# A transformer's cross-attention on one core: where a query's logits bank, a grouped output's projection and a norm's squares stand in the order of work

## The chip, the cores and the metric

The kernel runs on one core of one Trainium2 chip. The metric is the device time of one execution in microseconds; the median of three runs is used. PE is the matrix engine (its weight loads are shown as PEld), DVE the vector engine, ACT the scalar engine, POOL the general engine, SP the queue that issues most transfers.

## The reference

Four cross-attention layers follow each other on x (4 batches, 512 rows, 256 wide), all with the same context (4 batches, 1024 rows, 512 wide). Layers 0, 2 and 3 are alike: 16 heads of 64, a bias of -20 on some key columns by two masks, and a residual. Layer 1 is grouped: an RMS norm first, 16 query heads of 16 wide that share 4 key heads.

```python
def masked_layer(x, ctx):                 # layers 0, 2, 3
    q, k, v = x @ Wq, ctx @ Wk, ctx @ Wv  # 16 heads of 64
    logits = q k^T / 8 + col_bias
    return softmax(logits) v @ Wo + bo + x

def grouped_layer(x, ctx):                # layer 1
    xn = x * rsqrt(mean(x * x) + 1e-5) * norm_w
    q, k, v = xn @ wq, ctx @ wk, ctx @ wv # 16 and 4 heads of 16
    return x + softmax(q k^T / 4) v @ wo
```

## The kernel before

**Units and steps.** Each layer of a batch is cut into eight units: two heads of a masked layer, or half of four query heads of the grouped one. `order()` lays the 96 masked units out one to a step, and the 32 grouped units of layer 1 beside some of them: in steps 11 to 18, 21 to 28, 31 to 38 and 67 to 74. In the main loop (line 953) `g` is the step's masked unit, `lam` its grouped unit, `g1` the masked unit of the step before, `follows` and `coming` the masked and grouped units of the next step, `soon` the grouped unit of the step after that. A step with `lam` is called a grouped step here. Of a run's eight grouped units, two after each other (`h` 0 and 1) make one output; when the second is done, it is put in `turned` and in the next step's outputs.

**A step's work.** The scores of `g` come first (line 622): for eight blocks of 128 keys PE makes logits (L632, in the first block the bias too, L638), ACT copies them to SBUF (L642), DVE keeps a running maximum (L646) in the bank of the first block. DVE then reduces that maximum (L683 to L716), and spreads it over a pair of banks (`max_everywhere`, L723). The attention of `g1` (L662) is PE's next work. In a grouped step it is cut in four, and behind each quarter stand the second logits of `lam` (`exponentials_pair`, L611 on PE, L619 on ACT): the first ones were made in the step before by `maxima_pair` (L611, L601 and L603), and `lower_queries` (L709) took their maximum off the queries. DVE meanwhile works out the reciprocal sums of `g1` (L791 to L803), the normalised grouped output if `turned` has one (L779 to L785), and scales the output of `g1` (L814).

**What is woven in.** The rest of a step's PE work is in the list `fill`, with an estimated time for each item: output projections (L829, whose addition to x is DVE's L851), query projections (L543, scaled by ACT in L549 or, grouped, L553 with a transfer each in L554), the attention of `lam`, key projections (L467, grouped L485; ACT copies them out in L472 and L492), the norm (L575, L582, L586, L565 to L590), the context's transposes, and values (L509, L521). A clock `now` adds these estimates up. The subtractions of the maximum (L728 on DVE) and the exponentials (L734 on ACT) are events with due times on that clock; an item's own ending on ACT or DVE is issued behind the events that are due. The maxima pairs of `coming` have due times too, and are put ahead of the next item when these have passed. `behind_exponentials` issues all events that are left, and the normalisation of `g1` where that was put off.

```python
        now = 0.0
        for us, w in fill:
            while pairs and pairs[0][0] <= now:
                pair(pairs.pop(0)[1])
                now += 1.0
                pairs = [(max(at, now + 1.6), i) for at, i in pairs]
            done = w()
            now += us
            if callable(done):
                pass_events(now)
                done()
```

**Banks.** All eight banks of PSUM are handed out by `Place` (line 96). It takes the bank, or the even-odd pair, that was given back first, counted by returns in the order of the program; `back(late=n)` counts a bank as given back n returns later. A single bank whose partner is free counts two later. A matmul into a bank waits until the bank's last reader is done.

[...]

Of the kernel before, what the change touches and what calls it, by code (L numbers as in the profile page):

```python
# [20 lines left out]
NT = T // P  # L21
# [55 lines left out]
def kernel(ctx: ExitStack, tc: tile.TileContext, a: dict, out: bass.AP):  # L77
# [8 lines left out]
    def t_(shape, tag, name, bufs=1, dtype=FP):  # L86
        return sb.tile(shape, dtype, tag=tag, name=name, bufs=bufs)
# [31 lines left out]
    def st_slot(n):  # L119
        return st_all[:, n // (NT + 1), n % (NT + 1), :]  # L120
# [197 lines left out]
    def new_state(l, b):  # L318
        x_at[l, b] = x_free.pop(0)
        xs[l, b] = x_all[:, x_at[l, b]]  # L320
        return xs[l, b]

    def drop_state(l, b):
        x_free.append(x_at[l, b])
# [131 lines left out]
    def k_part(g, n, part):  # L456

        if not g.masked:
            return k_grouped(g, n, part)
        if n == 0 and part == 0:  # L460
            g.kt = t_([P, T], "kt", f"kt_{g.name}", bufs=2)
        if part == 0:
            g.k_place = Place(1)
        w = g.k_place
        m = w.ap
        for k in (2 * part, 2 * part + 1):
            nc.tensor.matmul(  # L467
                m, lhsT=g.wk[:, k, :], rhs=ctx_t[g.b][:, k, n * 512 : (n + 1) * 512],
                start=(k == 0), stop=(k == KT - 1),
            )  # L470
        if part:
            return lambda: (nc.scalar.copy(g.kt[:, n * 512 : (n + 1) * 512], m), w.back())  # L472
# [60 lines left out]
    def project_q(g):  # L533
        if g.masked:
            g.qt = t_([P, S], "qt", f"qt_{g.name}", bufs=2)
        else:
            g.qts = [t_([P, S], f"qt1{i}", f"qt1{i}_{g.name}", bufs=2) for i in range(2)]
            g.qt = g.qts[0]
        x = xs[g.l, g.b] if g.masked else gq[g.b, "xn"]
        w = Place(1)  # L540
        m = w.ap
        for k in range(KC):
            nc.tensor.matmul(m, lhsT=g.wq[:, k, :], rhs=x[:, k, :], start=(k == 0), stop=(k == KC - 1))  # L543
        if g.masked and g.last:
            drop_state(g.l, g.b)

        def evacuate():
            if g.masked:
                nc.scalar.mul(g.qt, m, 0.125)  # L549
            else:  # L550
                for h in range(2):
                    here, there = (slice(64 * i, 64 * (i + 1)) for i in (h, 1 - h))
                    nc.scalar.mul(g.qts[h][here, :], m[here, :], 0.25)  # L553
                    nc.scalar.dma_start(out=g.qts[h][there, :], in_=g.qts[h][here, :])  # L554
            w.back()

        return evacuate

    def reciprocal_rows(out_, in_, room):


        turned = room[:, 0:S]
        short = t_([P, S // 32, 1], "short", f"short{len(turns)}")
        turns.append(0)
        nc.vector.transpose(turned, in_)  # L565
        nc.vector.reciprocal(short, turned.rearrange("p (c r) -> p c r", r=32)[:, :, 0:1])
        nc.vector.transpose(
            out_.rearrange("p (c r) -> p c r", r=32), short.to_broadcast([P, S // 32, 32])
        )
# [3 lines left out]
    def norm_square(b):  # L573
        gq[b, "xn"] = t_([P, KC, S], "xn", f"xn{b}")
        nc.scalar.activation(gq[b, "xn"], xs[1, b], AF.Square)  # L575

    def rms_norm(b, room):
        x, xn, nw = xs[1, b], gq[b, "xn"], columns["L1_xattn_norm_w"]
        w = Place(1)
        m = w.ap  # L580
        for k in range(KC):
            nc.tensor.matmul(m, lhsT=ones, rhs=xn[:, k, :], start=(k == 0), stop=(k == KC - 1))  # L582

        def evacuate():
            inv = t_([P, S], "stage", f"inv{b}")
            nc.scalar.activation(inv, m, AF.Sqrt, bias=eps, scale=1.0 / C)  # L586
            w.back()
            reciprocal_rows(inv, inv, room)
            for k in range(KC):
                nc.vector.scalar_tensor_tensor(  # L590
                    xn[:, k, :], x[:, k, :], nw[:, k : k + 1], inv, ALU.mult, ALU.mult
                )

        return evacuate
# [222 lines left out]
    def project_out(g):  # L817
        x, acc = xs[g.l, g.b], xs.get((g.l + 1, g.b))
        opens = acc is None
        if opens and g.masked:  # L820
            acc = new_state(g.l + 1, g.b)
        elif opens:

            acc = xs[g.l + 1, g.b] = x
            x_at[g.l + 1, g.b] = x_at[g.l, g.b]
        w = Place()
        m = w.ap
        for k in range(KC):
            nc.tensor.matmul(  # L829
                m[:, k * S : (k + 1) * S], lhsT=g.wo[:, k * P : (k + 1) * P], rhs=g.ot,  # L830
                start=True, stop=True,
            )
        y = m.rearrange("p (k q) -> p k q", q=S)

        def add_last(q):
            nc.vector.tensor_tensor(acc[:, :, q], y[:, :, q], acc[:, :, q], ALU.add)

        def add():
            if g is masked[-1]:
                for i in range(0, NI, 2):  # L840
                    add_last(slice(i * P, (i + 2) * P))
                    store(g.b, range(i, i + 2))
                left[g.b] = -1
            elif opens and g.masked:
                bo = columns[f"L{g.l}_xattn_bo"]
                for k in range(KC):
                    nc.vector.scalar_tensor_tensor(
                        acc[:, k, :], y[:, k, :], bo[:, k : k + 1], x[:, k, :], ALU.add, ALU.add
                    )
            else:  # L850
                nc.vector.tensor_tensor(acc, y, x if opens else acc, ALU.add)  # L851
            w.back()

        left[g.b] -= 1
        return add
# [85 lines left out]
    def keys(of):  # L941
        return [(1.7, lambda h=h, part=part: k_part(of, h, part)) for h in range(2) for part in range(2)]
# [5 lines left out]
    count = 0  # L948
# [4 lines left out]
    for n in range(len(steps) + 2):  # L953
        g, lam = at(n)
        follows, coming = at(n + 1)
        soon = at(n + 2)[1]
# [29 lines left out]
        outs, ready = ready, []  # L986
        events = []
        late = []
# [6 lines left out]
        def behind_exponentials():  # L995
            pass_events(99.0)
            while late:
                late.pop(0)()
# [15 lines left out]
        queries = []  # L1014
# [19 lines left out]
        if turned or lam and g1:  # L1034

            w = Place(1)
            if lam and g1:
                reciprocal_sums(g1, w.ap)
            for each in turned:
                normalise_grouped(each, w.ap)  # L1040
            w.back()
        turned.clear()
        if lam:
            for i in range(NT // 2):
                if g1:
                    attend(g1, range(2 * i, 2 * i + 2))
                if coming and not g:
                    pair(i)
                exponentials_pair(lam, i)
                if i == 0 and g:  # L1050
                    g.mx_place.back()
                if not g:
                    if i == 1 and outs:
                        project_out(outs.pop(0))()
                    if i == 2 and queries:
                        project_q(queries.pop(0))()
            if g1:
                scale_out(g1)
                ready.append(g1)
            if g:  # L1060
                max_everywhere(g)
        elif g1 and g:
            attend(g1)
            if not ending:
                late.append(lambda: normalise(g1))
        elif g1:
            attend_last(g1)
            adds = [project_out(each) for each in outs]
            outs = []
            reciprocal_rows(g1.ot, g1.psum, g1.mx)  # L1070
            scale_out(g1)
            for add in adds:
                add()
# [9 lines left out]

        fill = [(1.8, lambda each=each: project_out(each)) for each in outs]
        outs = []
        of_queries = [(1.7, lambda each=each: project_q(each)) for each in queries]
        if lam:

            fill[0:0] = of_queries[0:1]
            fill += of_queries[1:]
        else:
            fill += of_queries
        if lam:

            def attend_grouped():
# [8 lines left out]
        for of in kk:  # L1106
            fill += keys(of) if of else []
        if soon and soon.first:
            fill += keys(soon)
        if follows and follows.l and follows.u == 0:  # L1110
            fill.append((1.7, lambda: project_q(follows)))
        if soon and soon.first:

            def norm():
                behind_exponentials()
                norm_square(soon.b)
                return rms_norm(soon.b, st_slot((NT + 1) * (count % 2) + NT))

            fill.append((1.7, norm))
        fill += [(1.0, rest) for rest in rests]  # L1120
        if coming and coming.first:
            fill += values(coming)
# [60 lines left out]
```

## Time and profile before

| what | value |
|---|---|
| runs of the kernel | 3748.72, 3751.1 (median), 3751.64 us |
| the profiled execution | 3749.48 us |
| its span | 3747.7 us |
| granted clock of PE | 0.996 |
| busy: PE, PEld, DVE, ACT, POOL | 98%, 49%, 81%, 56%, 43% |
| transfers | 98.59 MB, 26 GB/s over the span |

The span runs from the first to the last instruction of the profiled execution. A step can be read off the timeline from its first L632 to the next step's. A plain step takes 31.94 us (from 1788.51, for one); the grouped steps that begin at 1517.02 and 1562.81 take 45.79 and 51.64 us. The former finds nothing in `turned`, the latter does.

### The profile page before, as it was taken

Reading aid. Unit: us, or ns where it says so; the run is one execution under the profiler, and the core shown is the slowest. Engines: PE = TensorE matmul, PEld = TensorE weight load, DVE = VectorE, ACT = ScalarE, POOL = GpSimd, SP = SyncE. Lnnn points to the kernel's source line nnn. Section 1 sums busy time; section 2 is a strip of 40 time slices with the busy share of each in tenths; the row PEclk is TensorE's granted clock in tenths of the full one; section 3 lists DMA queues with packets and bytes.
Section 4 is the critical chain, followed back from the end, with each engine's and each line's share of the span. In section 5 each row is a group of like instructions: output and inputs, shape, how many; then the busy total and the mean of one; then the engine's idle time right before and its main releaser. Section 6 shows DMA issues by size and latency. Waiting matters only on the chain.

```text
span 3747.7 us, 48412 instructions
## 1 busy us (share of the span) xinstructions
PE 3683.2 (98%) x18606; PEld 1836.7 (49%) x18606; DVE 3025.1 (81%) x3959; ACT 2109.2 (56%) x2433; POOL 1625.9 (43%) x749
## 2 busy tenths in 40 slices
PE   8999999999999999999999999999999999999998
PEld 4555544445444454444555555554544445555554
DVE  6887788877888778887788878888788877888887
ACT  4555566555555555555555655555555555555554
POOL 3555433343333433334455555555333344555554
PEclk9999999999999999999999999999999999999999
DMA  2111110001000010000000110000100000000100
GB/s 68 43 32 25 40 30 22 18 20 25 22 22 18 21 25 22 19 21 18 26 26 26 48 37 26 26 23 22 25 22 22 18 24 26 26 26 26 31 25 8
DMA packets 187868, 98.59 MB, mean 26 GB/s; under 512 B 43240, under 2 KB 183528, under 8 KB 187636
## 3 DMA queue, kind: packets, MB, share of 16 engines
q1 hardware_dynamic: 182510, 82.90, 8.0%
q0 software_dynamic: 2560, 8.39, 0.8%
q10 hardware_dynamic: 2566, 4.20, 0.5%
q8 instruction: 147, 2.41, 0.3%
q14 instruction: 85, 0.70, 0.1%
HBM read 89.16 MB, written 2.10 MB: 24 GB/s over the span
## 4 chain that ended last, share of the span: by engine, by line
PE 89%; DVE 8%; ACT 1%; issue 1%; DMA 0%; POOL 0%; DVEq 0%; ACTq 0%; POOLq 0%
PE ps L509 19%; PE ps L662 18%; PE ps L467 17%; PE ps L632 15%; PE ps L611 6%; PE ps L829 5%; PE ps L543 5%; DVE ps L646 4%; DVE st L728 1%; ACT st L642 1%; PE ps L485 1%; PE ps L638 1%; DVE quarter L683 1%; DVE ps L683 0%; PE ps L373 0%
## 5 line engine op out<-in xcount | busy, mean ns | idle before, releaser
L773 POOL TENSOR_TENSOR st<-st 128x1024 f32<-128x1024 f32 x668 | 1581.2, 2367 | 2059.6 <-ACT st L734 2015.4
L646 DVE TENSOR_TENSOR ps<-ps,st 128x1024 f32<-128x1024 f32 x672 | 828.6, 1233 | 483.4 <-ACT st L642 422.1
L734 ACT ACTIVATE st<-st 128x1024 f32<-128x1024 f32 x768 | 788.4, 1055 | 668.6 <-DVE st L728 652.1
L728 DVE TENSOR_TENSOR st<-st,ps 128x1024 f32<-128x1024 f32 x768 | 886.3, 1216 | 3.2
L662 PE MATMUL ps<-st,v 128*64 128x512 f32 x4064 | 810.9, 598 | 0.0
L509 PEld LDWEIGHTS ps<-wv,ctx 128*128 128x128 f32 x6400 | 729.4, 192 | 80.9 <-issue 63.8
L642 ACT COPY st<-ps 128x1024 f32<-128x1024 f32 x768 | 713.1, 1049 | 68.6 <-PE ps L638 67.5
L509 PE MATMUL ps<-wv,ctx 128*128 128x128 f32 x6400 | 744.8, 276 | 0.6 <-ACT st L642 0.6
L632 PE MATMUL ps<-qt,kt 64*128 64x512 f32 x3072 | 702.5, 596 | 0.3 <-ACT st L642 0.3
L467 PE MATMUL ps<-ctx,wk 128*128 128x512 f32 x1536 | 694.9, 600 | 2.2 <-ACT ctx L379 2.2
L662 PEld LDWEIGHTS ps<-st,v 128*64 128x64 f32 x4064 | 231.2, 130 | 551.5 <-issue 460.5
L467 PEld LDWEIGHTS ps<-ctx,wk 128*128 128x128 f32 x1536 | 286.6, 191 | 398.0 <-issue 375.0
L632 PEld LDWEIGHTS ps<-qt,kt 64*128 64x128 f32 x3072 | 284.5, 186 | 324.4 <-ACT st L642 155.6
L521 ACT COPY v<-ps 128x512 f32<-128x512 f32 x200 | 117.3, 586 | 540.9 <-PE ps L509 537.0
L603 DVE TENSOR_TENSOR st<-st,ps 128x1024 f32<-128x1024 f32 x224 | 273.6, 1221 | 118.7 <-ACT st L601 65.9
L619 ACT ACTIVATE st<-ps 128x1024 f32<-128x1024 f32 x256 | 248.2, 1021 | 155.3 <-PE ps L611 114.9
L611 PE MATMUL ps<-qt,kt 32*128 32x512 f32 x2048 | 308.0, 639 | 3.2 <-DVE ot L814 3.2
L829 PE MATMUL ps<-ot,wo 128*128 128x512 f32 x448 | 218.2, 614 | 11.1 <-issue 10.3
L543 PE MATMUL ps<-x,wq 128*128 128x512 f32 x384 | 186.8, 609 | 16.6 <-DVE ot L785 15.5
L611 PEld LDWEIGHTS ps<-qt,kt 32*128 32x128 f32 x2048 | 93.2, 183 | 179.1 <-ACT st L619 51.9
L472 ACT COPY kt<-ps 128x512 f32<-128x512 f32 x192 | 110.3, 574 | 93.2 <-PE ps L467 92.3
L829 PEld LDWEIGHTS ps<-ot,wo 128*128 128x128 f32 x448 | 79.8, 190 | 141.2 <-issue 134.8
(142 smaller groups left out, 1573.3 us busy)
## 6 DMA issues: line engine op xcount, KB each, us to landing
wk<-in_L_xattn_Wk_dram SPq DMA_DIRECT2D x96, 256.0 KB
wv<-in_L_xattn_Wv_dram SPq DMA_DIRECT2D x96, 256.0 KB
wq<-in_L_xattn_Wq_dram SPq DMA_DIRECT2D x96, 128.0 KB
wo<-in_L_xattn_Wo_dram SPq DMA_DIRECT2D x96, 128.0 KB
qt<-qt ACTq DMA_DIRECT2D x32, 128.0 KB
xraw<-in_x_dram SPq DMA_DIRECT2D x3, 512.0 KB
out_dram<-out SPq DMA_DIRECT2D x3, 512.0 KB
wq<-in_L_xattn_wq_dram SPq DMA_DIRECT2D x32, 32.0 KB
```

Source lines behind the costliest of these rows:

```text
L467: nc.tensor.matmul(m, lhsT=g.wk[:, k, :], rhs=ctx_t[g.b][:, k, n * 512 : (n + 1) * 512], start=(k == 0), stop=(k == KT - 1),)
L509: nc.tensor.matmul(m[:, t * P : (t + 1) * P], lhsT=ctx_t[g.b][:, k, (4 * n + t) * P : (4 * n + t + 1) * P], rhs=g.wv[:, k, :], start=(k == ...
L543: nc.tensor.matmul(m, lhsT=g.wq[:, k, :], rhs=x[:, k, :], start=(k == 0), stop=(k == KC - 1))
L611: nc.tensor.matmul(ws[odd].ap[:, j * S : (j + 1) * S], lhsT=g.kt[rows, i * P : (i + 1) * P], rhs=g.qt[rows, :], start=True, stop=True,)
L632: nc.tensor.matmul(m[:, j * S : (j + 1) * S], lhsT=g.kt[g.rows[j], keys], rhs=g.qt[g.rows[j], :], start=True, stop=t > 0,)
L642: nc.scalar.copy(g.st[t], m)
L646: nc.vector.tensor_tensor(top, top, g.st[t], ALU.max)
L662: nc.tensor.matmul(g.po[at, :], lhsT=g.v[:, t, rows], rhs=g.st[t][:, j * S : (j + 1) * S], start=(t == first), stop=(t == last),)
L728: nc.vector.tensor_tensor(g.st[t], g.st[t], g.mb, ALU.subtract)
L734: nc.scalar.activation(st, st, AF.Exp)
L773: nc.gpsimd.tensor_tensor(g.acc, g.st[0] if t == 1 else g.acc, g.st[t], ALU.add)
L829: nc.tensor.matmul(m[:, k * S : (k + 1) * S], lhsT=g.wo[:, k * P : (k + 1) * P], rhs=g.ot, start=True, stop=True,)
```

## The change

Three things are moved.

First, in grouped steps the first query projection is issued directly behind the last of the second logits, before the output of `g1` is scaled and before `max_everywhere` takes its banks; it is no longer the first item of `fill`, and adds nothing to `now`. With it, the bank in which the reciprocal sums and the normalised grouped output are worked out is given back with `late=12`.

Second, in the step behind a run of grouped steps (19, 29, 39 and 75), the projection of the grouped output that was normalised in that step is put behind the keys, and behind the query.

Third, in the four steps with a norm (9, 19, 29 and 65) the squares are issued behind the third of the four grouped key parts, with the events that are left ahead of them; the norm's matmul stays behind the keys, and in steps 19 and 29 behind the moved projection.

```diff
-            w.back()
+            w.back(late=12)
         turned.clear()
...
                     if i == 2 and queries:
                         project_q(queries.pop(0))()
+            if g and queries:
+                project_q(queries.pop(0))()
             if g1:
                 scale_out(g1)
                 ready.append(g1)
...
-        fill = [(1.8, lambda each=each: project_out(each)) for each in outs]
+        fill, of_grouped = (
+            [(1.8, lambda each=each: project_out(each)) for each in outs if lam or each.masked == m]
+            for m in (True, False)
+        )
+        if lam:
+            of_grouped = []
         outs = []
         of_queries = [(1.7, lambda each=each: project_q(each)) for each in queries]
-        if lam:
-
-            fill[0:0] = of_queries[0:1]
-            fill += of_queries[1:]
-        else:
-            fill += of_queries
+        fill += of_queries
...
         if soon and soon.first:
-            fill += keys(soon)
+            def square():
+                behind_exponentials()
+                norm_square(soon.b)
+            of_keys = keys(soon)
+            fill += of_keys[:3] + [(0.0, square)] + of_keys[3:]
+        fill += of_grouped
         if follows and follows.l and follows.u == 0:
             fill.append((1.7, lambda: project_q(follows)))
         if soon and soon.first:
-            def norm():
-                behind_exponentials()
-                norm_square(soon.b)
-                return rms_norm(soon.b, st_slot((NT + 1) * (count % 2) + NT))
-            fill.append((1.7, norm))
+            fill.append((1.7, lambda: rms_norm(soon.b, st_slot((NT + 1) * (count % 2) + NT))))
```

## Prediction

> **What bounds the kernel now.** I read the page's busy times first, then the waits of PE, then the timeline step by step.
>
> ```profile
> PE 3683.2 (98%) x18606; PEld 1836.7 (49%) x18606; DVE 3025.1 (81%) x3959; ACT 2109.2 (56%) x2433; POOL 1625.9 (43%) x749
> ```
>
> PE sets the end; only 3747.7 - 3683.2 = 64.5 us are left in which it idles. The change removes no matmul, so all it can give is a part of these, and all it can take is new waits. PE's waits (line, releaser: total us, times, longest):
>
> ```profile
> PE ps L543 <- DVE ot L785: 15.5, 10, 1.6
> PE ps L829 <- issue: 10.3, 4, 2.6
> PE ps L582 <- ACT xn L575: 6.9, 4, 1.7
> ```
>
> These are the three things that the change speaks of: a query projection (L543) in a bank that the normaliser (L785) still reads; a grouped output's projection (L829) that needs the normalised output; the norm's matmul (L582) behind its squares. From start to start of matmuls in the timeline, where 128x512 ones follow each other every 0.43 us, they cost 1.77 us (12 times with two under "issue", one of them 1.2: 20.8 in all), 2.74 us (4 times: 11.0) and 1.90 us (4 times: 7.6). I use these.
>
> A step with a grouped unit ("grouped step"), timeline, first where the last step finished a grouped pair ("turned" is set):
>
> ```profile
> 537.57 0.69 DVE L785 TENSOR_TENSOR ot<-o,ps 128x512 f32<-128x512 f32 x1
> ...
> 538.32 1.98 PE L543 MATMUL ps<-x,wq 128*128 128x512 f32 x4 [1.58 <-DVE ot L785]
> ...
> 540.14 3.60 PE L829 MATMUL ps<-ot,wo 128*128 128x512 f32 x8
> ```
>
> and one where it is not:
>
> ```profile
> 489.98 1.25 DVE L723 STREAM_TRANSPOSE ps<-every 128x1024 f32<-128x1024 f32 x1
> ...
> 490.17 1.94 ACT L619 ACTIVATE st<-ps 128x1024 f32<-128x1024 f32 x2 [1.01 <-PE ps L611]
> ...
> 491.82 1.88 PE L829 MATMUL ps<-ot,wo 128*128 128x512 f32 x4
> ```
>
> To see here: the second logits' last exponential ends at 492.11, 0.29 us after the output projection starts, and DVE's L723 starts before either of the last two exponentials is done.
>
> [...] the trace has 1.28 us before the root (L586), but no load before the square (L575), so moving the square adds none.
>
> **The change, part by part.**
>
> *1. Banks of the query (late=12, query ahead of scale_out).* PE's order stays: the query was the first of fill already. Only the bank changes. I followed the allocator by hand through a turned and an unturned step. Before, the query takes the single bank that reciprocal_sums just gave back; L723 takes the oldest pair (sixth exponential), the output projection the pair of the seventh. After, that single bank counts twelve returns later, so the query takes half of the oldest pair, which ACT has read. Gain: 12 x 1.73 = 20.8 us.
>
> But a pair is now broken up, so each later taker moves on by one: L723 gets the seventh exponential's pair, the output projection the eighth's. PE then waits until 492.11 + 0.06 instead of 491.82: 0.35 us, and as much in turned steps (eighth exponential 538.77, projection due at 538.4). 32 x 0.35 = 11.2 us lost. L723 waits from 489.98 to 491.2; behind it on DVE stand eight subtractions, the output addition, keep_odd and the maxima. The last subtraction ends at about 503.3 (eight at 1.15 us, one addition); the first maxima pair, which takes its bank, is due at 504.5 to 504.9: covered. Without that cover it costs up to 1.2 us a step (rival D).
>
> *2. The 1.7 us that vanish from fill's clock.* The query no longer counts in `now`, so maxima pairs, due at 12.0 + 2.5 i, come one item later, and events one item later too. In turned steps that helps: in six of them the first pair waits 0.7 us for the last subtraction (pair to next key matmul 1.75 instead of 1.05): 6 x 0.7 = 4.2 us gained. In unturned steps it hurts. By fill's costs (1.8 output, 3.6 attend, four keys at 1.7) the fourth pair now has one value item behind it, not two. Before:
>
> ```profile
> 512.47 1.14 PE L611 MATMUL ps<-qt,kt 32*128 32x512 f32 x8
> ...
> 517.31 1.13 PE L632 MATMUL ps<-qt,kt 64*128 64x512 f32 x4
> ...
> 519.35 0.75 DVE L709 SCALAR_TENSOR_TENSOR qt<-ps,row,qt 128x512 f32<-128x512 f32 x1
> ```
>
> From the fourth pair (512.47) to the end of L709 (520.10) it is 7.63 us of PE, then DVE. The next scores' fourth block, which takes L709's bank in nearly all these steps, is due 4.84 + 2.89 = 7.73 us after the pair: just in time. With one value item (1.9 us) less it is due at 5.85. If it takes that bank, scores end 1.8 us late; if it takes another and the fifth block takes it, 0.97 us (one step of before, at 615.5, has this order and loses 0.6). The three unturned steps with maxima and no second query in each of four runs: 12 x 1.35 (middle) = 16.2 us lost; 11.6 to 21.6. Eight other grouped steps come to the old margin of 0.1 us: 0.2 each, 1.6 (0 to 4.8).
>
> Sum of 1 and 2: -20.8 - 4.2 + 11.2 + 16.2 + 1.6 = +4.0 us (-3 to +14).
>
> *3. Grouped output behind the keys (steps 19, 29, 39, 75).* PE goes on with query and keys while DVE normalises (L785 ends 2.7 us after the turn of the first projection; the keys alone give 6.9). Step 19: -2.74. Step 29 has 1.8 us of further bank waits beside it (48.9 us against 47.2 for the same items): -3.5 (2.7 to 4.5). Step 39: the same 1.8 us, but the first value item then comes at the bank of the second key half 0.7 us early: -3.7. Step 75 goes the other way:
>
> ```profile
> 3080.10 3.12 PE L829 MATMUL ps<-ot,wo 128*128 128x512 f32 x4 [2.58 <-issue]
> ...
> 3085.58 5.74 DVE L728 TENSOR_TENSOR st<-st,ps 128x1024 f32<-128x1024 f32 x5
> ...
> 3090.46 1.88 PE L543 MATMUL ps<-x,wq 128*128 128x512 f32 x4
> ```
>
> There the next item, project_q(follows), opens layer 2 of the same batch and reads the x that this output completes. By then fill's clock has issued all eight subtractions ahead of the addition (L851), which ends at about 3091.4; the query starts there, not at 3090.46, though PE could at 3085.9. +1.0 (0 to +2). Sum: -8.9 us (-7 to -11).
>
> *4. Squares amid the keys (steps 9, 19, 29, 65).* Before, ACT's key copy (0.69) and square (1.05) follow the last key part, then PE starts: 1.9 us. After, the square stands ahead of that copy, and 1.7 us of key matmuls lie beside it. ACT's exponentials end at 834.2, before the third part (835.9 to 837.6), so the square is done near 837.9 and L582 due at 839.4. Gain 4 x 1.9 = 7.6 us (6 to 7.6). The late normalise goes to DVE one item earlier: nothing waits. If ACT were behind, the second key copy would be too; nobody needs it before the next step.
>
> **Queues.** No DMA is moved: grouped queries keep their two on ACT's queue (L554) directly behind their scaling; SP's weight loads stand between steps; POOL's sums only follow exponentials that come at most 1.2 us later, and POOL is busy 43%.
>
> **Sum.** +4.0 - 8.9 - 7.6 = -12.5, call it -13 us. On the profiled execution: 3749.5 - 13 = 3736.5 (its span of 3747.7 and 1.8 around). That execution lies 1.6 us under the median, so on the median 3751.1 - 13 = 3738. The likeliest case's own range is 3731 to 3745.
>
> **Rivals.**
> - A, forecast: new waits take the place of the query's. 3738, chance 0.55.
> - B, one or both new waits don't appear (the blocks find other banks). Without L709's, -13 - 17.8 = -31: 3720; without the eighth exponential's, -24: 3727; without both, 3710. For it: each hangs on bank numbers, and ties decide some. Against: there are only four pairs, and the scores use all within four blocks. Chance 0.20.
> - C, losses at their upper ends and waits like L611 on L814 (three of 1.25 us now, by luck of banks) come more often: +10 on A, about 3748, no change to speak of. Chance 0.16.
> - D, slower: L723's 1.2 us reach PE at the first maxima pair, in the 20 unturned steps: 20 x 1.2 = 24, 3762. It breaks even at 0.65 us a step and is measurable from 1.0. For it: in turned steps that pair waits on just this subtraction today. Against: the pair comes 1.7 us later now, and 1.2 to 1.6 us of margin remain. Chance 0.09.
> - That the query keeps its bank is excluded: twelve returns exceed the nine between.
>
> **Numbers.** A measurement of this kernel can tell some 0.2% (7.5 us) from no change. Faster: A but its edge (0.51) and B (0.20), 0.71; same: that edge and C, 0.20; slower 0.09. The range takes in C and B but for its end: 3720 to 3749.
>
> **What would show it.** L543 on L785 gone from PE's waits; L829 on L619 in 32 steps at 0.3 us; the scores (L632) waiting on L709 in 12 steps; grouped steps in pairs as long as now (97.4 us for 45.79 + 51.64); step 9 and 65 shorter by 1.9, step 19 by 4.6, step 29 by 5 to 6; step 75 longer by 1, with its query waiting on L851. It is wrong if pairs of grouped steps shorten by over 1 us or lengthen by over 3.

## The result: no difference that can be measured, and the profile after

The changed kernel takes 3748.6 us (median of 14 runs, 3746.54 to 3749.53), the kernel before 3749.97 us in as many runs beside it. The ratio is 0.9995, with a 95% interval of 0.9987 to 1.0003. The interval takes in 1, so not even the sign of a difference is shown. The forecast of 3738 is missed by 11 us; the measured time lies 0.4 us inside the upper end of the range, where case C stood.

What the change set out to remove is gone. PE's waits in the changed kernel (line, releaser: total us, times, longest):

```profile
PE ps L632 <- DVE qt L709: 6.4, 7, 1.7
PE ps L829 <- ACT st L619: 5.5, 32, 0.2
PE ps L543 <- ACT st L734: 5.3, 1, 5.3
PE ps L632 <- ACT st L642: 4.7, 14, 0.3
```

None of the three lines of before is left. In their place stand the scores behind L709, the output projection behind the eighth exponential (32 times, as many as there are grouped steps) and one query that waits 5.3 us. The page shows how little such sums tell: PE's busy time rose from 3683.2 to 3694.7 us with the same 18606 matmuls. In L632 alone it rose from 702.5 to 714.3 us, with 3072 matmuls in both, so a part of the new waits shows as busy time.

```profile
PE 3694.7 (99%) x18606; PEld 1842.0 (49%) x18606; DVE 3033.9 (81%) x3959; ACT 2105.5 (56%) x2433; POOL 1624.2 (43%) x749
```

So I compare step by step, from a step's first L632 to the next one's. The steps not named here agree within 0.1 us.

| steps | before to after, us |
|---|---|
| 32 grouped steps, sum | +12.4 |
| of these, with something in turned (12) | -0.3 |
| 9 and 65 (squares alone) | -3.6 |
| 19 (both) | -4.6 |
| 29 and the step behind it (both) | -6.7 |
| 39 and 40 (grouped output) | -3.0 |
| 75 and 76 (grouped output) | +3.9 |
| all | -1.6 |

The span fell by 3.0 us (the profiled execution after is the fastest of its fourteen); the rest lies before the first step and in the last one and behind it, which the change leaves alone. The new waits, in the timeline of the changed kernel. First an unturned step:

```profile
488.59 1.94 ACT L619 ACTIVATE st<-ps 128x1024 f32<-128x1024 f32 x2 [1.01 <-PE ps L611]
...
489.64 1.26 DVE L723 STREAM_TRANSPOSE ps<-every 128x1024 f32<-128x1024 f32 x1 [1.48 <-ACT st L619]
...
490.58 1.98 PE L829 MATMUL ps<-ot,wo 128*128 128x512 f32 x4 [0.17 <-ACT st L619]
```

L723 starts when the first of the last two exponentials is done (489.6), L829 when the second is (490.53). Then the start of the turned step behind it:

```profile
513.11 1.14 PE L611 MATMUL ps<-qt,kt 32*128 32x512 f32 x8
514.18 2.05 PE L509 MATMUL ps<-wv,ctx 128*128 128x128 f32 x16
...
516.16 1.13 PE L632 MATMUL ps<-qt,kt 64*128 64x512 f32 x4
...
520.00 0.75 DVE L709 SCALAR_TENSOR_TENSOR qt<-ps,row,qt 128x512 f32<-128x512 f32 x1
...
520.89 4.56 PE L632 MATMUL ps<-qt,kt 64*128 64x512 f32 x20 [1.67 <-DVE qt L709]
```

One value item (16 matmul records) now stands between the fourth maxima pair and the scores, not two, and the fourth block waits until L709 has let its bank go: 7.64 us behind the pair, as before.

### The profile page after: what moved, and what is told of

Its sections match the earlier page's. It is cut to its first block, busy times and chain, and to the rows that moved or that the text cites. A ratio compares the mean times of both kernels' runs of the same rounds, so it can differ in the third digit from the quotient of the medians.

```text
span 3744.7 us, 48356 instructions
## 1 busy us (share of the span) xinstructions
PE 3694.7 (99%) x18606; PEld 1842.0 (49%) x18606; DVE 3033.9 (81%) x3959; ACT 2105.5 (56%) x2433; POOL 1624.2 (43%) x749
## 4 chain that ended last, share of the span: by engine, by line
PE 90%; DVE 6%; ACT 2%; issue 1%; DMA 0%; POOL 0%; DVEq 0%; ACTq 0%; POOLq 0%
PE ps L662 20%; PE ps L509 19%; PE ps L467 17%; PE ps L632 16%; PE ps L611 8%; PE ps L829 5%; PE ps L543 3%; DVE ps L646 2%; DVE st L728 1%; ACT st L642 1%; ACT st L619 1%; PE ps L485 1%; PE ps L638 1%; DVE quarter L683 1%; DVE st L603 0%
## 5 line engine op out<-in xcount | busy, mean ns | idle before, releaser
L734 ACT ACTIVATE st<-st 128x1024 f32<-128x1024 f32 x768 | 783.0, 1054 | 706.3 <-DVE st L728 695.0
L509 PE MATMUL ps<-wv,ctx 128*128 128x128 f32 x6400 | 752.8, 277 | 1.2 <-ACT st L642 0.6
L632 PE MATMUL ps<-qt,kt 64*128 64x512 f32 x3072 | 714.3, 598 | 11.1 <-DVE qt L709 6.4
L467 PE MATMUL ps<-ctx,wk 128*128 128x512 f32 x1536 | 685.6, 597 | 2.2 <-ACT ctx L379 2.2
L632 PEld LDWEIGHTS ps<-qt,kt 64*128 64x128 f32 x3072 | 290.4, 186 | 340.9 <-ACT st L642 155.1
L619 ACT ACTIVATE st<-ps 128x1024 f32<-128x1024 f32 x256 | 248.1, 1021 | 158.5 <-PE ps L611 119.4
L611 PE MATMUL ps<-qt,kt 32*128 32x512 f32 x2048 | 304.6, 639 | 3.3 <-DVE ot L814 3.3
L829 PE MATMUL ps<-ot,wo 128*128 128x512 f32 x448 | 218.8, 615 | 6.2 <-ACT st L619 5.5
L611 PEld LDWEIGHTS ps<-qt,kt 32*128 32x128 f32 x2048 | 92.0, 183 | 159.1 <-ACT st L619 51.9
L829 PEld LDWEIGHTS ps<-ot,wo 128*128 128x128 f32 x448 | 77.0, 189 | 146.6 <-issue 110.4
L723 DVE STREAM_TRANSPOSE ps<-every 128x1024 f32<-128x1024 f32 x96 | 120.8, 1258 | 32.2 <-ACT st L619 24.8
```

Source lines behind the costliest of these rows:

```text
L467: nc.tensor.matmul(m, lhsT=g.wk[:, k, :], rhs=ctx_t[g.b][:, k, n * 512 : (n + 1) * 512], start=(k == 0), stop=(k == KT - 1),)
L509: nc.tensor.matmul(m[:, t * P : (t + 1) * P], lhsT=ctx_t[g.b][:, k, (4 * n + t) * P : (4 * n + t + 1) * P], rhs=g.wv[:, k, :], start=(k == ...
L611: nc.tensor.matmul(ws[odd].ap[:, j * S : (j + 1) * S], lhsT=g.kt[rows, i * P : (i + 1) * P], rhs=g.qt[rows, :], start=True, stop=True,)
L632: nc.tensor.matmul(m[:, j * S : (j + 1) * S], lhsT=g.kt[g.rows[j], keys], rhs=g.qt[g.rows[j], :], start=True, stop=t > 0,)
L734: nc.scalar.activation(st, st, AF.Exp)
L829: nc.tensor.matmul(m[:, k * S : (k + 1) * S], lhsT=g.wo[:, k * P : (k + 1) * P], rhs=g.ot, start=True, stop=True,)
```

## The experiments

Theory: in grouped steps the gain is eaten by two things that come with it, the item that fell out of fill's clock and the bank that moved on by one; in step 75 it is eaten by the query that needs the moved output. Rivals: the banks do it all, or DVE's subtractions bind the turned steps whatever else is changed. Each kernel was timed beside the kernel before; a ratio is to that kernel, with its interval. "Half speed" means matmuls that follow each other at 853 ns in place of 429 (those of the values, 128 wide, at 213 in place of 112), at a granted clock of 0.50 in the traces of both kernels; the last section shows where it came.

**e1_squares: the squares alone**, in the kernel before.

```diff
-            fill += keys(soon)
+            of_keys = keys(soon)
+            fill += of_keys[:3] + [(0.0, square)] + of_keys[3:]
...
-            fill.append((1.7, norm))
+            fill.append((1.7, lambda: rms_norm(soon.b, st_slot((NT + 1) * (count % 2) + NT))))
```

> The kernel before with the squares amid the keys alone. The theory (the parts add up, each read from its own steps of the two traces): steps 9, 19, 29 and 65 shorter by 1.8 us each, the time 7.2 us under the kernel before (ratio 0.9981). The rival (the gain is given back later in the step): under 2 us.

3740.17 us against 3749.67, ratio 0.9974 (0.9965 to 0.9984). L582's wait on L575 is gone, and steps 9 and 65 are shorter by 1.8 us each, as in the changed kernel. The profiled steps 29, 39 and 75 gained 1.7 more each and step 19 lost 1.7, though nothing but the squares of 19 and 29 moved in them: this is half speed, which is there in one execution and not in another. Step 10 is 1.5 us longer for the same reason: its context transposes and values follow each other at 213 ns in place of some 110. The squares' new place brings ACT no further table load: the kernel before and the changed one have nine each, of 1.28 us, four of them before the root (L586) and none before the square. The gain is real and of the expected size within the interval.

**e2_grouped: the grouped output behind the keys alone**, and **e8_grouped_late: with the bank's mark.** e2 has the two hunks of `of_grouped` alone; e8 has this as well:

```diff
-            w.back()
+            w.back(late=0 if lam else 12)
         turned.clear()
```

> The kernel before with the grouped output's projection behind the keys alone, in steps 19, 29, 39 and 75. The theory: step 19 shorter by 2.8, 29 by 4.5, 39 by 3.7, step 75 longer by 3.2 because project_q(follows) waits on the addition L851 and then runs its matmuls at half speed; some 7 us less in all (ratio 0.9981). The rival (in step 75 it is a bank, as the bank is not marked late here): step 75 not longer, 11 us less.

> The kernel before with the grouped output's projection behind the keys, and late=12 in steps without a grouped unit alone; the query stays first in fill in grouped steps. The theory (in e2_grouped the next item behind the first projection took the bank that L785 was still reading, so the wait only changed its place): steps 19, 29 and 39 shorter by 2.8 to 4.5 us each, step 75 longer by 3; L467 and L543 on L785 gone from these steps; some 5 us under e2_grouped's time. The rival (the gain in these steps needs the query's move as well): as e2_grouped.

e2 took 3746.13 us, ratio 0.9989 (0.9981 to 0.9997), half of what the theory gave. PE's waits show why:

```profile
PE ps L543 <- DVE ot L785: 20.6, 12, 2.5
PE ps L467 <- DVE ot L785: 5.1, 2, 2.5
```

Without the mark, the next item takes the very bank in which DVE normalises. In steps 39 and 75 that is the first key part, in 19 and 29 the query; each waits 2.5 us for L785 in place of the projection, and step 39 gains nothing (38.15 against 38.17 us). Step 75 is 1.6 us longer nonetheless, so e2's rival doesn't hold either. e8 took 3739.69 us, ratio 0.9973 (0.9963 to 0.9984), 10.6 us under the kernel before, where e2 had 3.5. So this part needs `late=12`, but not the query's move. In step 19 e8 gains 4.5 us, more than the 2.8 expected: the projection, now ahead of the norm's matmul, covers the squares too (L582 waits in two steps, not four). The two last parts of the change thus overlap in steps 19 and 29: there the squares' move adds less than 0.1 us to what e8 gains (42.59 us in the changed kernel, 42.68 in e8, in both steps). Step 75 is longer by 2.5 us here as well.

**e3_query: the query ahead and late=12 alone.**

```diff
-            w.back()
+            w.back(late=12)
...
+            if g and queries:
+                project_q(queries.pop(0))()
...
-        if lam:
-            fill[0:0] = of_queries[0:1]
-            fill += of_queries[1:]
-        else:
-            fill += of_queries
+        fill += of_queries
```

> The kernel before with the query ahead and late=12 alone. The theory: grouped steps longer by 12 us in all, time 12 us over the kernel before (ratio 1.0032), with L543 on L785 gone, L632 on L709 in 12 steps by 0.9 to 1.9 us, L829 on L619 in 32 steps by 0.3. The rival (the loss in the changed kernel comes from the three parts together, through the order of the banks): within 3 us of the kernel before.

3764.47 us, ratio 1.0038 (1.0025 to 1.0052). The grouped steps are 12.4 us longer, as in the changed kernel to the tenth of a microsecond. Of the rest of the 14.8 us, step 19 has 1.5 (half speed), and steps 40 and 76 have 0.7 and 0.6 (their scores). The part of the change that its first words name makes the kernel slower by itself.

**e4_clock: the clock restored in all grouped steps**, in the changed kernel.

```diff
         queries = []
+        spent = 0.0
...
             if g and queries:
+                spent = 1.7
                 project_q(queries.pop(0))()
...
-        now = 0.0
+        now = spent
```

> The changed kernel, but fill's clock starts at 1.7 in grouped steps whose query went ahead. The clock theory: the scores' waits on L709 go (21 us in 20 steps), while the first maxima pair of six turned steps waits some 2 us for the last subtraction (12 us back): 5 to 9 us under the changed kernel. The bank theory (late=12 and the half pair make the loss, the clock has no part): as the changed kernel within 2 us, scores as late as there.

3746.03 us, ratio 0.9991 (0.9982 to 0.9999), 2 to 3 us under the changed kernel: neither figure, but the clock theory's mechanism. The scores' waits on L709 are gone; in seven turned steps they still come 0.6 to 0.8 us late. Yet the turned steps with a second query came out at the length of before (51.63 against 51.64 us; step 13 is 1.6 us longer, by half speed), since the wait went to the first maxima pair and to the key part that shares its place:

```profile
PE ps L611 <- DVE st L728: 2.4, 6, 0.8
PE ps L467 <- DVE st L728: 2.3, 6, 0.8
```

```profile
546.63 4.60 DVE L728 TENSOR_TENSOR st<-st,ps 128x1024 f32<-128x1024 f32 x4
...
549.42 1.13 PE L611 MATMUL ps<-qt,kt 32*128 32x512 f32 x4
...
551.28 1.13 PE L611 MATMUL ps<-qt,kt 32*128 32x512 f32 x4 [0.74 <-DVE st L728]
551.34 2.00 ACT L734 ACTIVATE st<-st 128x1024 f32<-128x1024 f32 x2
551.47 0.69 DVE L676 TENSOR_TENSOR o<-o,ps 64x512 f32<-64x512 f32 x1 [0.24 <-ACT o L672]
```

The first half of the pair starts at 549.42, the second only at 551.28: its bank is that of the spread maximum, and DVE's last subtraction ends at 551.23. PE reached this point earlier by what the query had saved, and waited there instead. This speaks for the rival that DVE binds these steps; e5 decides.

**e5_mixed: the clock restored in unturned steps alone.**

```diff
+        full = bool(turned)
...
-                spent = 1.7
+                spent = 0.0 if full else 1.7
```

> The changed kernel, but fill's clock starts at 1.7 in those grouped steps alone that find nothing in turned. The theory (in unturned steps the missing 1.7 us brings the wait on L709 in the next step, in turned steps it makes room for the last subtraction): turned steps lose their late scores and keep their first maxima pair free of waits, 49 us instead of 51.5; the 20 unturned ones stay at 0.43 us over the kernel before; 18 us under the changed kernel, about 3730. The rival (turned steps are bound by DVE's subtractions whatever the clock says, as they came out at the length of before when the clock was restored everywhere): turned steps stay at 51.6, the time within 4 us of the changed kernel.

3728.84 us, ratio 0.9943 (0.993 to 0.9957): 20 us under the changed kernel. Turned steps take 50.03 us (with a second query) instead of 51.5, and their scores are on time. The rival falls: DVE binds the place of the pair, not the step. In the kernel before, in e4 and in e5 alike, DVE's last subtraction ends 34.2 us into such a step, and the key part behind the first pair starts at 35.3 (step 25, for one). What differs is how much PE has done by then: in e5 one key part more.

**e6_late: the bank marked in turned steps alone**, on top of e5.

```diff
-            w.back(late=12)
+            w.back(late=12 if full else 0)
```

> As e5_mixed, and the bank is marked late in steps alone that find something in turned. The theory (the 0.43 us of an unturned step are the wait of the output projection for the eighth exponential, which comes from the mark): unturned steps fall back to 45.79 us, L829 on L619 falls from 32 to 12 times; 8.6 us under e5_mixed, about 3721. The rival (the 0.43 us come from the place of the query ahead of scale_out): unturned steps stay at 46.2, no gain.

3719.96 us, ratio 0.9921 (0.9907 to 0.9934). The unturned steps are back at 45.79 us (28 and 38 alone stay 0.6 us over the kernel before), and PE's waits have

```profile
PE ps L543 <- ACT st L734: 5.3, 1, 5.3
...
PE ps L829 <- ACT st L619: 2.1, 12, 0.2
```

with L829 on L619 down from 32 to 12. So the 0.43 us of an unturned step come from the mark, which sends the query to half of a pair; the query's place in the code costs nothing there.

**e7_opening: the query that opens a layer ahead of the last value item**, on top of e6.

```diff
         fill += of_grouped
+        opening = []
         if follows and follows.l and follows.u == 0:
-            fill.append((1.7, lambda: project_q(follows)))
+            opening.append((1.7, lambda: project_q(follows)))
+        if not of_grouped:
+            fill += opening
...
             fill += values(masked[g.n + 1])
+        if of_grouped:
+            fill[-1:-1] = opening
```

> As e6_late, and in steps 39 and 75 project_q(follows) stands ahead of the last value item instead of right behind the grouped output's projection. The theory (in step 75 this query waits for the addition L851 behind eight subtractions, and PE then runs at half speed for 2 us): step 75 falls from 41.3 to about 34 us, 7 us under e6_late, about 3714. The rival (what it waits for comes later too, or the query is then late for the next scores): step 75 and 76 together over 70 us.

3712.17 us, ratio 0.9898 (0.9883 to 0.9913). Step 75 fell from 41.6 us in e6 to 33.8, and with step 76 it takes 66.5 us, so the rival falls. Its end in the changed kernel:

```profile
3076.05 8.00 DVE L728 TENSOR_TENSOR st<-st,ps 128x1024 f32<-128x1024 f32 x7
...
3078.10 1.88 PE L829 MATMUL ps<-ot,wo 128*128 128x512 f32 x4
...
3083.97 1.22 DVE L851 TENSOR_TENSOR x<-ps,x 128x1024 f32<-128x1024 f32 x1
...
3085.29 3.75 PE L543 MATMUL ps<-x,wq 128*128 128x512 f32 x4 [5.31 <-ACT st L734]
```

and in e7:

```profile
3052.34 1.88 PE L829 MATMUL ps<-ot,wo 128*128 128x512 f32 x4
...
3054.06 5.52 PE L509 MATMUL ps<-wv,ctx 128*128 128x128 f32 x48
...
3058.21 1.22 DVE L851 TENSOR_TENSOR x<-ps,x 128x1024 f32<-128x1024 f32 x1
...
3059.48 1.98 PE L543 MATMUL ps<-x,wq 128*128 128x512 f32 x4
```

In the changed kernel the projection's matmuls are over at 3079.98, and L851 starts at 3083.97, as the seven subtractions that the program lists ahead of it end (8.00 us from 3076.05). The addition comes as long after the projection as before, but three value parts fill that time. The first of these fences has a trap: the wait is put down to ACT's L734, which ended at 3085.14, while L851, whose x the query reads, ended at 3085.19, 0.1 us ahead of the matmul. e7 changes only what stands between L851 and the query, and the wait went.

## Why the prediction was right and wrong

| term | predicted | measured |
|---|---|---|
| waits of the query and of the first maxima pair that go | -25.0 | -22.0 |
| output projection behind the eighth exponential, 32 steps | +11.2 | +13.4 |
| scores behind L709, 12 steps | +16.2 | +17.0 |
| scores of eight other grouped steps | +1.6 | +4.2 |
| grouped steps | +4.0 | +12.4 |
| steps 9, 19, 29, 39, 65, 75 and those behind them | -16.5 | -14.0 |
| all | -12.5 | -1.6 |

The first is from e6: 12 turned steps gained 17.1 us while they still paid 0.41 each. The rest is from the changed kernel's steps: 0.42 us each; scores later by 17.0 us in sum; 0.6 us in seven of the eight steps. The four rows add up to 12.6, within 0.2 us of the grouped steps' own sum.

**Banks: right, each wait where it was put.** L723 waits for the seventh exponential and the output projection for the eighth, as the count of banks had it, and the query no longer waits for L785. The term "0.35 us" measured 0.42. The 1.2 us by which L723 is late stayed hidden, so rival D did not come.

**The clock: right in kind.** The scores are late by 0.9 us in five of the twelve steps and by 1.2 to 2.1 in the others, depending on which block gets L709's bank; the middle taken was fair. Mis-sized was "eight other grouped steps come to the old margin of 0.1 us: 0.2 each": with the margin that thin, the fourth block took the bank of the first copy in seven of them and waited for ACT, 0.6 us each.

**Gains too high by 3 us.** I added the query's 1.73 us and the pair's 0.7 us as if each stood alone. e6 shows turned steps with a second query 1.61 us shorter with 0.41 still paid: 2.0 us, not 2.4, where both waits had been. They can't be added, since the pair ends at a moment that DVE sets: in the kernel before, e4 and e6 the key part behind it starts at the same 35.3 us. What e6 gains is the key part that now stands ahead of this moment, and 0.2 us of wait stay at the pair.

**Step 75: the term outside its range.** "+1.0 (0 to +2)". The query's start was met, 30.2 us into the step, as predicted. What came on top was not in the sum: its four matmuls ran at half speed (853 ns from start to start), and so did the first five of the values behind them (213 ns in place of 112), at a granted clock of 0.50 from 3082.93 to 3089.76 us; and in step 76 the scores came 0.6 us later. Together +3.9. The prediction put nothing down for half speed, though its own fence of this step has it: four matmuls in 3.12 us where the others take some 1.9.

**Steps 29 and 39: the right size from a wrong cause.** I called 1.8 us there "further bank waits". They are half-speed matmuls behind the 2.7 us wait (853 ns from start to start in both, at a granted clock of 0.50). With the wait they went, which made step 29 better than forecast (-6.7 with the squares, against -5.4). Step 39's first value item waited for the second key copy, as predicted (0.58 us on L472), and step 40 lost 0.7 us by its banks.

**The case was wrong, and the range held by its edge.** What was forecast is A, with 0.71 for "faster"; what came is "no difference", which had 0.20. A's own range, 3731 to 3745, doesn't take in the 3748.6; the whole range does because it was drawn out to C, so the hit is owed to its width more than to the sum. Half of C's reasons came, larger losses; more waits of L611 on L814 did not (three, as before). Of the 10.9 us between the sum's -12.5 and -1.6, the grouped steps have 8.4, with gains put 3.0 too high and losses 5.6 too low; step 75 has 2.9, and step 29 takes 1.3 off. e7, with the same three moves but without most of what they bring with them, is 38 us or 1.0% under the kernel before.

## What to carry to other kernels

Where a planner lays work out by estimated times, an item that is pulled out of the list must still be paid for on its clock, and whether that helps is to be asked of each kind of step by itself: here the shift was worth 1.6 us in one kind and cost up to 2.1 in the scores behind the other. A mark that steers one buffer away from one consumer moves every later one on as well; put it only where the wait is. Before work is moved behind other work, look at what reads its result next, and count the queue ahead of that result on the engine that makes it.

## What the runs showed of the hardware that was not expected

In some profiles a wait of PE had a price behind it: 1.7 us in step 19 of e1, none in that step of the kernel before. The same projection after the same wait of 2.58 us, first in the kernel before, then in e1:

```profile
821.91 1.96 PE L829 MATMUL ps<-ot,wo 128*128 128x512 f32 x4 [2.58 <-issue]
```

```profile
821.81 3.60 PE L829 MATMUL ps<-ot,wo 128*128 128x512 f32 x4 [2.58 <-issue]
```

In the second, the matmuls follow each other at 853 ns instead of 429, for about 1.7 us in excess; then the speed is back. The granted clock of the same stretch was 1.00 in the first and 0.59 in the second (its length, busy time of the five engines with their instructions, granted clock, transfers):

```profile
821.00:825.00 4.00, 3.09 (x8) 1.44 (x9) 3.97 (x5) 1.06 (x1) 0.00 (x0) 1.00 0.00 0
```

```profile
821.00:825.00 4.00, 3.19 (x4) 1.51 (x5) 3.98 (x4) 1.06 (x1) 0.00 (x0) 0.59 0.00 0
```

In the kernel before, the granted clock was 0.50 for 3.41 us from each of 1295.59, 1770.04 and 3080.76 us, behind this wait in steps 29, 39 and 75. In the changed kernel it was 0.50 for 6.83 us from 3082.93 us, in step 75. In the rest of steps 1 to 94 it was 1.00 in both.

From the last matmul's start to the next, the waits for a grouped output's normalisation are gaps of 3.12 to 3.17 us. In the profiles of before, e1, e2 and e3 there are 16, and half speed follows in 11: in the kernel before in steps 29, 39 and 75 but not in 19, in e1 in step 19 but not in the other three. It follows in all five of the gaps of 5.90 us (step 75 of the changed kernel, e4, e5, e6 and e8). It came elsewhere too: in step 10 of e1, e5, e6 and e7 and in step 13 of e4. What decides between the cases was not shown.

So the same work took different times: up to the end of step 10 the changed kernel and e5 have the same instructions, and step 10 takes 48.78 us in one and 50.23 in the other. In these profiles a wait of 2.7 us cost up to 4.5, with 1.8 us of half speed behind it, and half speed followed each of the five waits of more than 5 us.
